# Attention over the scales: the second image's means and columns mostly on GpSimd, and a written-out ending for the last two items

## The chip, the cores and the metric

One core of a Trainium2 chip runs the whole program. The metric is the device time of one execution in microseconds (us). The engines are PE (TensorE), DVE (VectorE), ACT (ScalarE), POOL (GpSimd) and SP, which issues DMAs. Each works through its own instructions in order, and waits on semaphores for what other engines produce.

## The reference, cut to what matters

The program is four layers on an image batch of 2 x 128 x 64 x 64 in float32: a block of state-space layers, two attention layers over 4096 pixels, and an attention over scales. Only the last is changed:

```python
for i, scale in enumerate((1, 2, 4, 8)):
    if scale > 1:
        xs = x.reshape(b, c, h // scale, scale, w // scale, scale).mean(axis=(3, 5))
        f = bilinear_resize(conv3x3(xs, conv_w[i], conv_b[i]), h, w)
    else:
        f = conv3x3(x, conv_w[i], conv_b[i])
    feats.append(f)
xr = jnp.stack(feats, axis=1).transpose(0, 3, 4, 1, 2).reshape(b * h * w, 4, c)
qkv = xr @ attn_in_w.T + attn_in_b
q, k, v = (heads(t) for t in jnp.split(qkv, 3, axis=-1))      # 8 heads
scores = jnp.einsum('nhqd,nhkd->nhqk', q, k) / jnp.sqrt(jnp.float32(hd))
o = jnp.einsum('nhqk,nhkd->nhqd', softmax(scores), v)
res = o.transpose(0, 2, 1, 3).reshape(-1, 4, c) @ attn_out_w.T + attn_out_b + xr
normed = layernorm(res) * ln_g + ln_b                         # over the 128 channels
fused = normed.reshape(b, h, w, 4, c).transpose(0, 3, 4, 1, 2).reshape(b, 4 * c, h, w)
out = jnp.einsum('bchw,oc->bohw', fused, fus_w) + fus_b[None, :, None, None]
```

At every pixel four tokens, one for each scale, attend to each other, and a projection of all four gives the output.

## The kernel before, in words

The 128 channels lie on the partitions. The layer starts near 4233 us and runs to the end. An item is one image (b) and one of eight chunks of 512 pixels (c), so there are NI = 16 items, 0 to 7 of the first image and 8 to 15 of the second. The stage is under a manual schedule: each engine's order is the order in which the program issues. Nothing plans it; the function `period(n)` (L1273) writes it out by hand.

A period works on four items at once: o = n - 1 is normalised and fused, p = n gets its attention weights applied and its output mix, m = n + 1 its scores and soft maximum, r = n + 2 its features, convolution and projections. Some steps and their lines:

- `features(r)`, L1118: POOL makes the three coarse feature maps of a chunk from the columns `lo` and their vertical differences `di` (L1124, L1125, L1133, L1134).
- `conv(r)`, L1113: nine matmuls of the full-size convolution, in pieces along the period.
- `product` and `scores` of m: DVE multiplies k (PSUM) by q (L1157), PE sums over the heads (L1164).
- `weights` and `weighted` of p: for each key scale ti PE spreads the attention weights into a PSUM tile pw (L1199), and DVE multiplies it by v (L1206). `add_ov` (L1210) sums the four results: 0 + 1 on POOL after ti = 1, then 2 + 3 and 0 + 2 on DVE.
- `soft_max`, `soft_exp`, `soft_sum` of m (L1174 to L1192): DVE, ACT, DVE. They end in `at`.
- `mix_out(p)`: for each scale two matmuls into a po tile (L1219, L1220), which ACT evacuates twice, as the square sq (L1221) and as cen (L1222). The po, pqkv, pf and coarse-convolution tiles share one PSUM pool of three buffers.
- `variance`, `newton` and `factors` of p: PE sums the squares (pva, L1228), ACT takes logarithm, exponential and square (L1233, L1234, L1236), DVE (L1241), ACT (L1242) and DVE (L1243) refine the result, PE spreads it (prs, L1250). prs and pw are the same single buffer of four PSUM banks.
- `normalise` and `fuse` of the item before: DVE scales cen by prs (L1257), PE fuses the scales (pfus, L1264), ACT adds the bias (L1269), SP sends the chunk out (L1270).

Three steps are done once for an image, not for an item. `means(b)` (L1045): for scales 2, 4 and 8, DVE adds neighbouring columns into t1 (L1053, reading every second element) and neighbouring rows into sm (L1054), POOL clears the padded tile xs (L1056), ACT writes the scaled means into it (L1057). `coarse_conv` (L1060): nine matmuls on xs (L1069), ACT writes the result fl (L1075 or L1077). `columns(si)` (L1079): horizontal interpolation on DVE: differences df (L1085), copies at both edges (L1088, L1089), one multiply-add for each of the 2, 4 or 8 phases (L1092), the first and last row repeated (L1095, L1096), vertical differences di for scales 4 and 8 (L1100). For image 0 they run ahead of the periods. For image 1 they are put into periods by the table `extra`, whose hooks `more(k)` stand at fixed places of `period`: means in period 2 after soft_sum (hook 4), the coarse convolutions in periods 3 and 4 at hooks 1 and 3, the columns in period 5 at hook 4, ahead of mix_out.

prod, ov, sq, t1 and df take turns in six buffers of the tag "prod"; sm and fl of a scale share one buffer.

Periods run from n = -2 to 16. In the last two most steps have no item: period 15 normalises and fuses item 14 and applies the weights of item 15, period 16 normalises and fuses item 15.

Of the kernel before, what the change touches and what calls it, by code (L numbers as in the profile page):

```python
# [6 lines left out]
F32 = mybir.dt.float32  # L7
AF = mybir.ActivationFunctionType
ALU = mybir.AluOpType
# [4 lines left out]
B, C, H, W = 2, 128, 64, 64  # L14
N = H * W
P = 128
# [13 lines left out]
NS = len(SCALES)  # L30
# [37 lines left out]
def tile_conv_seq(ctx: ExitStack, tc, x, consts, vecs, wemb, wlay, wconv, wdt, wqkv, wsmall, wms, out):  # L68
    nc = tc.nc
# [46 lines left out]
    with tc.manual_schedule(), ExitStack() as s:  # L116
# [4 lines left out]
        sp = scans.enter_context(tc.tile_pool(name="l0s", bufs=1, side="right"))  # L121
# [91 lines left out]
        NI, NST, NSL = len(items), 8, 32  # L213
        st = [{} for _ in items]
# [3 lines left out]
        def has(i):  # L218
            return 0 <= i < NI
# [676 lines left out]
        sp = s.enter_context(tc.tile_pool(name="ats", bufs=1, reuse_waits="tile"))  # L896
        psa = s.enter_context(tc.tile_pool(name="atpa", bufs=2, reuse_waits="tile", space=PSUM))
        psm = s.enter_context(tc.tile_pool(name="atpm", bufs=1, reuse_waits="tile", space=PSUM))
        for now in range(NALL + LAG + 10):
            r, u = divmod(now, NU)  # L900
            w = now % 8
# [70 lines left out]
    with ExitStack() as s, tc.manual_schedule():  # L972
        sp = s.enter_context(tc.tile_pool(name="mss", bufs=1, reuse_waits="tile"))
# [50 lines left out]
        for si in (2, 3):  # L1024
            wgt[si] = sp.tile([P, SCALES[si]], F32, name=f"wgt{si}")
            for k in range(SCALES[si]):
                w = (k + 0.5) / SCALES[si] - 0.5
# [5 lines left out]
        NI = len(items)  # L1033
        st = [{} for _ in items]
        low = {}
        coarse = {}
# [6 lines left out]


        def means(b):  # L1045
            prev, off = xt[:, b], 1
            for si in range(1, NS):
                sc_ = SCALES[si]
                hh = H // sc_
                t1 = sp.tile([P, 2 * hh, hh], F32, name=f"t1_{si}", tag="prod", bufs=6)  # L1050
                sm = sp.tile([P, hh, hh], F32, name=f"sm_{si}", tag=f"fl{si}")
                e = off + 2 * hh
                nc.vector.tensor_tensor(t1, prev[:, off:e, off:e:2], prev[:, off:e, off + 1 : e : 2], ALU.add)  # L1053
                nc.vector.tensor_tensor(sm, t1[:, 0 : 2 * hh : 2, :], t1[:, 1 : 2 * hh : 2, :], ALU.add)  # L1054
                xs = coarse["xs", si] = sp.tile([P, hh + 2, hh + 2], F32, name=f"xs_{si}", tag=f"xs{si}")
                nc.gpsimd.memset(xs, 0.0)  # L1056
                nc.scalar.activation(xs[:, 1 : hh + 1, 1 : hh + 1], sm, AF.Copy, scale=1.0 / (sc_ * sc_))  # L1057
                prev, off = sm, 0

        def coarse_conv(si, r0):  # L1060
# [15 lines left out]
            else:  # L1076
                nc.scalar.activation(dst, src, AF.Identity, bias=v1("conv_b3", si))  # L1077

        def columns(si):  # L1079

            sc_ = SCALES[si]
            hh, half = H // sc_, sc_ // 2
            fl = coarse["fl", si]
            df = sp.tile([P, hh, hh - 1], F32, name=f"df_{si}", tag="prod", bufs=6)
            nc.vector.tensor_tensor(df, fl[:, :, 1:], fl[:, :, : hh - 1], ALU.subtract)  # L1085
            lo = sp.tile([P, hh + 2, W], F32, name=f"lo_{si}", tag=f"lo{si}")
            mid = lo[:, 1 : hh + 1, :]
            nc.vector.tensor_copy(mid[:, :, :half], fl[:, :, 0:1].to_broadcast([P, hh, half]))  # L1088
            nc.vector.tensor_copy(mid[:, :, W - half :], fl[:, :, hh - 1 : hh].to_broadcast([P, hh, half]))  # L1089
            for kk in range(half, half + sc_):  # L1090
                end = kk + sc_ * (hh - 2) + 1
                nc.vector.scalar_tensor_tensor(  # L1092
                    mid[:, :, kk:end:sc_], df, (kk + 0.5) / sc_ - 0.5, fl[:, :, : hh - 1], ALU.mult, ALU.add
                )
            nc.vector.tensor_copy(lo[:, 0, :], lo[:, 1, :])  # L1095
            nc.vector.tensor_copy(lo[:, hh + 1, :], lo[:, hh, :])  # L1096
            di = None
            if si > 1:
                di = sp.tile([P, hh + 1, W], F32, name=f"di_{si}", tag=f"di{si}")
                nc.vector.tensor_tensor(di, lo[:, 1:, :], lo[:, : hh + 1, :], ALU.subtract)  # L1100
            low[si] = lo, di


# [104 lines left out]
        def add_ov(eng, i, a, b):  # L1208
            o = st[i]["ov", a]
            eng.tensor_tensor(o, o, st[i].pop(("ov", b)), ALU.add)  # L1210
# [62 lines left out]
        def period(n, extra):  # L1273
            o, p, m, r = n - 1, n, n + 1, n + 2

            def do(i, f, *a):
                if has(i):
                    f(i, *a)

            def more(k):  # L1280
                for f, a in extra.get((n, k), ()):
                    f(*a)


            do(r, features)
            do(r, conv, (0, 1))
            for ti in range(NS):
                do(m, product, ti)
                if ti == 0:
                    do(o, normalise)  # L1290
                do(p, weights, ti)
                if ti + 2 < NS:
                    do(m, project, 1, ti + 2)
                if ti > 0:
                    do(m, scores, ti - 1)
                do(p, weighted, ti)
                if ti == 1 and has(p):
                    add_ov(nc.gpsimd, p, 0, 1)
                if ti == 0:
                    do(o, fuse, range(NS))  # L1300
                do(r, conv, ((), (2, 3), (4, 5), (6, 7))[ti])
                more(ti)
            do(m, scores, NS - 1)

            if has(p):
                add_ov(nc.vector, p, 2, 3)
                add_ov(nc.vector, p, 0, 2)
            do(m, soft_max)
            do(r, conv, (8,))
            do(r, conv_out)  # L1310
            for si in range(NS):
                do(m, project, 2, si)
            do(m, soft_exp)
            do(m, soft_sum)
            more(4)
            for si in range(NS):
                do(p, mix_out, si)
            more(5)

            do(p, variance)  # L1320
            for si in range(NS):
                if si == 2:
                    do(p, newton)
                do(r, project, 0, si)
            do(r, project, 1, 0)
            do(p, factors)
            do(r, project, 1, 1)
            more(6)

        means(0)  # L1330
        for r0 in (0, 16):
            coarse_conv(1, r0)
        coarse_conv(2, 0), coarse_conv(3, 0)
        for si in range(1, NS):
            columns(si)
        last = NCH - 3
        extra = {
            (last - 3, 4): [(means, (1,))],
            (last - 2, 1): [(coarse_conv, (1, 0))], (last - 2, 3): [(coarse_conv, (1, 16))],
            (last - 1, 1): [(coarse_conv, (2, 0))], (last - 1, 3): [(coarse_conv, (3, 0))],  # L1340
            (last, 4): [(columns, (si,)) for si in range(1, NS)],
        }
        for n in range(-2, NI + 1):
            period(n, extra)


# [79 lines left out]
```

## Time and profile before

| | us |
|---|---|
| median of 3 runs | 5029.0 (5028.12 to 5030.46) |
| profiled execution, its own time | 5032.79 |
| its span, first to last instruction | 5031.0 |
| PE busy | 4671.6 (93%) |
| DVE busy | 4024.3 (80%) |
| ACT busy | 2367.4 (47%) |
| POOL busy | 2309.9 (46%) |
| mean granted clock of PE | 0.948 of full speed |

A line of the timeline gives start, duration, engine, line of the program, operation, output <- inputs, sizes and a count of instructions; square brackets hold the idle time just ahead of it and what ended it. A line of windows gives, for a stretch of time, its length and each engine's busy time with its number of instructions, the granted clock, the share of DMA and the rate. Line numbers are those of the kernel before.

### The profile page before, as it was taken

To read this page: it belongs to the slowest core of one execution; us is meant where nothing else is said; L and a number is where in the kernel's file an instruction comes from. 1 tells how busy PE (TensorE), PEld (TensorE's weight loads), DVE (VectorE), ACT (ScalarE), POOL (GpSimd) and SP (SyncE) were. 2 spreads that over 40 slices of the span, in tenths; PEclk is the share of its full clock that TensorE was granted. 3 is DMA by queue.
4 is the path that set the end of the run, shared out by engine and by line. 5 is a ranking of instruction groups with operands and counts; after the bars stand their busy time and mean duration, and the time that the engine had idled before them with its cause. 6 is when DMAs were issued, how large, how long until landed. Compare 5 with 4: busy or idle time off the path is not lost.

```text
span 5031.0 us, 48923 instructions
## 1 busy us (share of the span) xinstructions
PE 4671.6 (93%) x14797; PEld 2244.9 (45%) x14797; DVE 4024.3 (80%) x4284; ACT 2367.4 (47%) x3221; POOL 2309.9 (46%) x1948
## 2 busy tenths in 40 slices
PE   5889999999988899899999999999999999999997
PEld 1222222222222222366667766666666666333332
DVE  6999999999999999788886677667766775767775
ACT  4677777777777777522222222333333332223332
POOL 3777776666777777513332233233333333323331
PEclk8898889988999989899999999999999999999998
DMA  6333333332333333224444344434443442000000
GB/s 162 68 68 69 69 71 71 71 68 63 71 68 68 72 71 70 62 65 108 109 110 126 105 112 110 117 98 110 114 100 97 112 111 70 5 5 7 7 7 7
DMA packets 242343, 386.24 MB, mean 77 GB/s; under 512 B 88592, under 2 KB 88992, under 8 KB 233632
## 3 DMA queue, kind: packets, MB, share of 16 engines
q1 hardware_dynamic: 192928, 315.94, 25.9%
q10 hardware_dynamic: 49152, 67.17, 5.4%
q8 instruction: 118, 1.93, 0.2%
q14 instruction: 145, 1.19, 0.1%
HBM read 101.02 MB, written 13.37 MB: 23 GB/s over the span
## 4 chain that ended last, share of the span: by engine, by line
PE 49%; POOL 24%; issue 12%; DVE 9%; ACT 2%; DMA 2%; SPq 1%; ACTq 0%; DVEq 0%; POOLq 0%
POOL h L410 19%; PE po L804 15%; PE pq L754 15%; PE pa L652 2%; PE pf L1113 2%; DVE tr L784 2%; PE pqkv L1140 2%; POOL dtu L370 1%; PE pw L1199 1%; POOL z L433 1%; PE pb L652 1%; PE pfus L1264 1%; PE psc L1164 1%; PE po L1220 1%; DVE prod L1157 1%
## 5 line engine op out<-in xcount | busy, mean ns | idle before, releaser
L791 POOL COPY pt<-tr 32x512 f32<-32x512 f32 x1024 | 649.0, 634 | 1440.2 <-DVE tr L784 711.7
L407 DVE TENSOR_TENSOR_SCAN h<-da,carry,h 128x512 f32<-128x512 f32 x1024 | 1241.6, 1266 | 59.9 <-ACT da L396 31.0
L410 POOL TENSOR_TENSOR h<-h,cb 128x2048 f32<-128x2048 f32 x256 | 1161.4, 4537 | 20.9 <-POOL carry L409 0.4
L754 PE MATMUL pq<-k,q 128*128 128x512 f32 x2048 | 962.8, 593 | 9.1 <-DVE sc L759 6.8
L804 PE MATMUL po<-pt,vt 128*128 128x256 f32 x4096 | 967.3, 379 | 2.8 <-DMA pt<-tr 2.8
L769 ACT ACTIVATE sc<-sc,nm 128x2048 f32<-128x2048 f32 x256 | 510.5, 1995 | 912.0 <-DVE nm L765 675.4
L759 DVE TENSOR_SCALAR_CACHE_REDUCE sc<-pq 128x1024 f32<-128x1024 f32 x512 | 625.0, 1222 | 366.7 <-PE pq L754 345.4
L804 PEld LDWEIGHTS po<-pt,vt 128*128 128x128 f32 x4096 | 779.1, 190 | 295.6 <-issue 208.3
L396 ACT ACTIVATE da<-dtb,am 128x512 f32<-128x512 f32 x1024 | 681.6, 684 | 231.1 <-DVE h L407 210.2
L389 DVE TENSOR_TENSOR h<-bb,pdu 128x2048 f32<-128x2048 f32 x256 | 581.8, 2273 | 85.8 <-PE py L422 29.3
L784 DVE STREAM_TRANSPOSE tr<-sc 128x2048 f32<-128x2048 f32 x256 | 591.7, 2311 | 63.2 <-DMA pt<-tr 53.9
L422 PE MATMUL py<-h,sel 128*32 128x512 f32 x2048 | 511.4, 643 | 1.6 <-POOL h L410 1.6
L754 PEld LDWEIGHTS pq<-k,q 128*128 128x128 f32 x2048 | 382.8, 190 | 284.8 <-issue 246.1
L383 PE MATMUL pdu<-dtu,fsel 128*128 128x512 f32 x512 | 325.3, 722 | 116.0 <-DVE h L389 113.8
L422 PEld LDWEIGHTS py<-h,sel 128*32 128x32 f32 x2048 | 115.2, 118 | 415.3 <-issue 409.9
L310 PE MATMUL pu<-xn,wu 128*128 128x512 f32 x512 | 246.7, 615 | 2.6 <-ACT xn L300 1.7
L383 PEld LDWEIGHTS pdu<-dtu,fsel 128*128 128x128 f32 x512 | 95.9, 214 | 321.8 <-DVE h L389 199.2
L409 POOL COPY carry<-h 128x4 f32<-128x4 f32 x256 | 47.5, 185 | 395.8 <-DVE h L407 393.9
L1206 DVE TENSOR_TENSOR ov<-v,pw 128x2048 f32<-128x2048 f32 x64 | 146.2, 2285 | 68.6 <-PE pw L1199 68.6
L1140 PE MATMUL pqkv<-f,ws 128*128 128x512 f32 x384 | 189.5, 618 | 3.0 <-DVE prod L1157 2.3
L1210 POOL TENSOR_TENSOR ov<-ov 128x2048 f32<-128x2048 f32 x16 | 72.6, 4536 | 257.7 <-DVE ov L1206 257.7
L370 POOL TENSOR_TENSOR dtu<-dt,u 128x1024 f32<-128x1024 f32 x32 | 75.1, 2346 | 191.9 <-ACT dt L364 191.9
(245 smaller groups left out, 5254.4 us busy)
## 6 DMA issues: line engine op xcount, KB each, us to landing
pt<-tr SPq DMA_DIRECT2D x2048, 64.0 KB, 2.0
dtb<-dt SPq DMA_DIRECT2D x1024, 64.0 KB, 2.0
pt<-tr ACTq DMA_DIRECT2D x1024, 64.0 KB, 2.2
bb<-dr SPq DMA_DIRECT2D x128, 256.0 KB, 4.4
cb<-dr SPq DMA_DIRECT2D x128, 256.0 KB, 4.7
uw<-ufold SPq DMA_DIRECT2D x12, 576.0 KB, 4.3
uw<-dkept SPq DMA_DIRECT2D x20, 288.0 KB, 3.0
xt<-in_x SPq DMA_DIRECT2D x16, 256.0 KB, 4.7
```

The lines of the kernel that those rows point to most:

```text
L383: nc.tensor.matmul(pdu, lhsT=four(s_ % 4), rhs=st[i]["dtu"][:, s_ // 4, :], start=True, stop=True)
L389: nc.vector.tensor_tensor(h, st[i]["bc", 0], pdu.unsqueeze(1).to_broadcast([P, 4, CH]), ALU.mult)
L396: nc.scalar.activation(da, st[i]["dtb", s_], AF.Exp, scale=am[items[i][1]][:, j, gg, m : m + 1])
L407: nc.vector.tensor_tensor_scan(h[:, m, :], da, h[:, m, :], carries[b, l][:, j, gg, m : m + 1], ALU.mult, ALU.add)
L410: nc.gpsimd.tensor_tensor(h, h, st[i]["bc", 1], ALU.mult)
L422: nc.tensor.matmul(py[r : r + 32, :], lhsT=sel, rhs=st[i]["h", s_ + k][:, m, :], start=(m == 0), stop=(m == 3), tile_position=(0, r),)
L754: nc.tensor.matmul(pq[:, i, :], lhsT=sta["q", r, grp][:, it * P : (it + 1) * P], rhs=sta["k"][:, at : at + CH], start=True, stop=True)
L759: nc.vector.tensor_scalar(dst, pq, 1.0, None, ALU.mult, ALU.max, accum_out=sta["mx"][:, c2 : c2 + 1])
L769: nc.scalar.activation(sc, sc, AF.Exp, bias=nm, scale=scale, accum_out=sm[:, hh : hh + 1])
L784: nc.vector.transpose(tr, sta.pop(("sc", r, blk, hh)).rearrange("p (t r f) -> p r t f", r=NB, f=32))
L791: nc.gpsimd.tensor_copy(dst, src)
L804: nc.tensor.matmul(sta["po", r, grp], lhsT=sta["vt"][:, jt, :], rhs=rhs, start=(jt == 0), stop=(jt == N // P - 1))
```

## The change

Three things. `means(1)` is wholly on POOL: its six sums, the clearing, and the three scales. `means(0)` stays as it was. `columns` is cut into three parts: part 0 makes the differences df and the edge copies, part 1 the interpolations, part 2 the edge rows and di. For image 1 parts 0 and 2 are on POOL and part 1 stays on DVE; they stand at hooks 3, 4 and 5 of period 5. For image 0 everything stays on DVE, now scale by scale through the three parts, in the order of before. And periods 15 and 16 are replaced by `ending`: period 14 no longer ends in factors(14); the four weights and weighted steps of item 15 come first, then factors, normalise and fuse of item 14, then item 15's additions on DVE, the last of them in four pieces of 512, its mix_out, variance, newton and factors, and its normalise in four pieces, each followed by its fuse matmul.

```diff
 def means(b):
+    eng = nc.gpsimd if b else nc.vector
...
-        nc.vector.tensor_tensor(t1, prev[:, off:e, off:e:2], prev[:, off:e, off + 1 : e : 2], ALU.add)
-        nc.vector.tensor_tensor(sm, t1[:, 0 : 2 * hh : 2, :], t1[:, 1 : 2 * hh : 2, :], ALU.add)
+        eng.tensor_tensor(t1, prev[:, off:e, off:e:2], prev[:, off:e, off + 1 : e : 2], ALU.add)
+        eng.tensor_tensor(sm, t1[:, 0 : 2 * hh : 2, :], t1[:, 1 : 2 * hh : 2, :], ALU.add)
...
-        nc.scalar.activation(xs[:, 1 : hh + 1, 1 : hh + 1], sm, AF.Copy, scale=1.0 / (sc_ * sc_))
+        if b:
+            nc.gpsimd.tensor_scalar(xs[:, 1 : hh + 1, 1 : hh + 1], sm, 1.0 / (sc_ * sc_), None, ALU.mult)
+        else:
+            nc.scalar.activation(xs[:, 1 : hh + 1, 1 : hh + 1], sm, AF.Copy, scale=1.0 / (sc_ * sc_))
...
-def columns(si):
+def columns(b, si, part):
+    eng = nc.gpsimd if b else nc.vector
...
+    if part == 0:
+        df = coarse["df", si] = sp.tile([P, hh, hh - 1], F32, name=f"df_{si}", tag="prod", bufs=6)
+        eng.tensor_tensor(df, fl[:, :, 1:], fl[:, :, : hh - 1], ALU.subtract)
+        lo = coarse["lo", si] = sp.tile([P, hh + 2, W], F32, name=f"lo_{si}", tag=f"lo{si}")
+        mid = lo[:, 1 : hh + 1, :]
+        eng.tensor_copy(mid[:, :, :half], fl[:, :, 0:1].to_broadcast([P, hh, half]))
+        eng.tensor_copy(mid[:, :, W - half :], fl[:, :, hh - 1 : hh].to_broadcast([P, hh, half]))
+        return
+    lo = coarse["lo", si]
+    if part == 1:
+        mid, df = lo[:, 1 : hh + 1, :], coarse.pop(("df", si))
+        for kk in range(half, half + sc_):
...
+                mid[:, :, kk:end:sc_], df, (kk + 0.5) / sc_ - 0.5, fl[:, :, : hh - 1], ALU.mult, ALU.add
...
+        return
+    eng.tensor_copy(lo[:, 0, :], lo[:, 1, :])
+    eng.tensor_copy(lo[:, hh + 1, :], lo[:, hh, :])
...
+        eng.tensor_tensor(di, lo[:, 1:, :], lo[:, : hh + 1, :], ALU.subtract)
...
-    do(p, factors)
+    if p != NI - 2:
+        do(p, factors)
...
+def ending():
+    o, p = NI - 2, NI - 1
+    for ti in range(NS):
+        weights(p, ti)
+        weighted(p, ti)
+        if ti == 1:
+            add_ov(nc.gpsimd, p, 0, 1)
+    factors(o)
+    normalise(o)
+    fuse(o, range(NS))
+    add_ov(nc.vector, p, 2, 3)
+    a, b = st[p]["ov", 0], st[p].pop(("ov", 2))
+    for si in range(NS):
+        nc.vector.tensor_tensor(a[:, si, :], a[:, si, :], b[:, si, :], ALU.add)
+    for si in range(NS):
+        mix_out(p, si)
+    variance(p)
+    newton(p)
+    factors(p)
+    w = st[p]
+    for si in range(NS):
+        nc.vector.tensor_tensor(w["cen"][:, si, :], w["cen"][:, si, :], w["prs"][:, si, :], ALU.mult)
+        fuse(p, (si,))
...
-    (last, 4): [(columns, (si,)) for si in range(1, NS)],
+    (last, 3): [(columns, (1, si, 0)) for si in range(1, NS)],
+    (last, 4): [(columns, (1, si, 1)) for si in range(1, NS)],
+    (last, 5): [(columns, (1, si, 2)) for si in range(1, NS)],
...
-for n in range(-2, NI + 1):
+for n in range(-2, NI - 1):
     period(n, extra)
+ending()
```

More of the change, by code (lines that the diff above doesn't have):

```diff
@@ L1083, in columns @@
             fl = coarse["fl", si]
[L1084 to L1096, printed above, removed]
+            if part == 0:
[10 more added lines that the diff above has]
+                for kk in range(half, half + sc_):
+                    end = kk + sc_ * (hh - 2) + 1
+                    nc.vector.scalar_tensor_tensor(
+                        mid[:, :, kk:end:sc_], df, (kk + 0.5) / sc_ - 0.5, fl[:, :, : hh - 1], ALU.mult, ALU.add
+                    )
+                return
+            eng.tensor_copy(lo[:, 0, :], lo[:, 1, :])
+            eng.tensor_copy(lo[:, hh + 1, :], lo[:, hh, :])
             di = None
@@ L1099, in columns @@
                 di = sp.tile([P, hh + 1, W], F32, name=f"di_{si}", tag=f"di{si}")
-                nc.vector.tensor_tensor(di, lo[:, 1:, :], lo[:, : hh + 1, :], ALU.subtract)
+                eng.tensor_tensor(di, lo[:, 1:, :], lo[:, : hh + 1, :], ALU.subtract)
             low[si] = lo, di
@@ L1334, in tile_conv_seq @@
         for si in range(1, NS):
-            columns(si)
+            for part in range(3):
+                columns(0, si, part)
         last = NCH - 3
```

## The prediction

> **What bounds the kernel now.** I read the page's chain of waits first, then windows between equal instructions of the last stage, then the single instructions where a window is long. Over the whole span the chain lies on PE for 49% and on POOL for 24%, but POOL's part is L410, in a stage that the change leaves alone. What counts is the last 800 us. There I cut windows from one item's variance matmul (L1228, pva) to the next: one turn of `period`.
>
> ```profile
> core 0: us, PE busy (x) PEld busy (x) DVE busy (x) ACT busy (x) POOL busy (x), PEclk, DMA share, GB/s
> 4334.05:4376.45 42.40, 41.37 (x147) 14.26 (x146) 31.43 (x20) 14.62 (x23) 13.17 (x14) 1.00 0.02 7
> 4376.45:4427.60 51.15, 43.44 (x147) 14.67 (x147) 36.47 (x26) 16.09 (x26) 15.36 (x18) 0.93 0.02 6
> 4578.19:4629.80 51.61, 44.52 (x147) 15.26 (x146) 42.72 (x48) 14.69 (x23) 14.65 (x14) 0.90 0.02 6
> 4968.85:5031.00 62.15, 34.94 (x97) 11.12 (x96) 21.07 (x12) 13.04 (x21) 4.51 (x1) 0.75 0.02 8
> ```
>
> The first row is an undisturbed period: PE is busy 41.37 of 42.40 us, so PE bounds it, and DVE and POOL have 11 and 29 us to spare. The second holds the second image's means: 8.75 more. The third holds its columns: 9.2 more (51.61 - 42.40). The fourth is the ending, with PE idle 27 us: a serial chain. These three rows are all that the change can win in.
>
> Means:
>
> ```profile
> 4412.76 1.02 PE L1220 MATMUL po<-ov,wc 128*128 128x512 f32 x2
> ...
> 4417.05 2.25 DVE L1053 TENSOR_TENSOR t<-xt 128x2048 f32<-128x2048 f32 x1
> ...
> 4420.65 1.61 ACT L1057 ACTIVATE xs<-sm 128x1024 f32<-128x1024 f32 x2 [6.70 <-DVE sm L1054]
> ...
> 4423.89 2.07 PE L1219 MATMUL po<-f,kc 128*128 128x512 f32 x2 [6.68 <-ACT cen L1222]
> ```
>
> ACT's first scale waits for DVE's sums with mix_out's evacuations queued behind it; they free PE's three po buffers, so PE idles 6.68 and comes back at half clock (2.07 against 1.02).
>
> Columns:
>
> ```profile
> 4576.38 1.15 DVE L1085 TENSOR_TENSOR df<-fl 128x992 f32<-128x992 f32 x1
> ...
> 4589.69 0.68 DVE L1241 SCALAR_TENSOR_TENSOR nt<-pva,nt 128x512 f32<-128x512 f32 x1
> ...
> 4591.91 2.09 PE L1250 MATMUL prs<-rs,kc 32*128 32x512 f32 x8 [7.09 <-DVE rs L1243]
> ```
>
> DVE works 13.4 us on columns; newton (L1241) stands behind. In the undisturbed period it starts 3.98 after pva, here 11.50, 7.5 late; PE waits 7.09 and loses 3.2 more in four groups at half clock (prs, pqkv, and pf 3.17 against 1.88).
>
> Ending:
>
> ```profile
> 4974.30 0.69 DVE L1243 TENSOR_TENSOR rs<-rs,nt 128x512 f32<-128x512 f32 x1 [0.79 <-ACT nt L1242]
> ...
> 4981.70 2.29 DVE L1206 TENSOR_TENSOR ov<-v,pw 128x2048 f32<-128x2048 f32 x1 [2.21 <-PE pw L1199]
> 4987.63 2.29 DVE L1206 TENSOR_TENSOR ov<-v,pw 128x2048 f32<-128x2048 f32 x1 [3.65 <-PE pw L1199]
> ...
> 4998.07 4.69 DVE L1210 TENSOR_TENSOR ov<-ov 128x2048 f32<-128x2048 f32 x2
> ...
> 5022.04 5.17 PE L1264 MATMUL pfus<-cen,wfus 128*128 128x512 f32 x8 [2.39 <-DVE cen L1257]
> ```
>
> One PSUM tile serves prs and pw, so PE and DVE alternate from 4975 to 4998.
>
> **What the Trainium skill says.** "SBUF — State Buffer", Who interferes with whom: a DVE instruction with two SBUF inputs and a GpSimd instruction that reads SBUF exclude each other for the whole instruction; with one SBUF input DVE is free of it. The trace agrees:
>
> ```profile
> 49.83 2.34 POOL L370 TENSOR_TENSOR dtu<-dt,u 128x1024 f32<-128x1024 f32 x1 [28.37 <-ACT dt L364]
> ...
> 49.96 2.62 DVE L202 SCALAR_TENSOR_TENSOR uhi<-raw,uhi 128x384 f32<-128x384 f32 x1
> ```
>
> L202 takes 2.62 where its neighbour of the same shape takes 0.56: it waited for POOL to end. L1206, one PSUM input, stays at 2.29 beside POOL. "TensorE: Matmul & The Clock Gate", Part 1: after an idle window of some 3.4 us the clock halves; the 2.09 for prs above, usually 1.14, agrees. "GPSIMD Engine Reference", 7: a read step above 8 bytes costs half more; the means step over 2 floats, 8 bytes, at the edge, and no row here shows that step on POOL.
>
> **Means, step by step.** Removed: DVE's six sums and ACT's three scales, and with them the 8.75. Added: the same nine instructions on POOL, after its add 0+1, which ends at 4401.6; POOL then has idle time until features at 4418 (and these wait some 20 us before a projection needs them). POOL's prices: L1210 4.54 for 2048, L370 2.35 for 1024, so 0.16 plus 2.14 ns an element. The first sum is 4.54 (bounds 4.54, since no row of this size is shorter, and 6.8 with the half of section 7; I take 4.54, the step being not above 8), the second 2.35, memset 1.06, the scale over 1024 between 1.6 (ACT's two together) and 3.4 (four times L1124's 0.86 for 256), I take 2.9. The rest is 3 us. All of it is hidden as work; the exclusion is not. The add 2+3 (L1210, two SBUF inputs) is ready at 4406.5. POOL's first sum ends at 4406.2 and its second holds until 4408.6; DVE adds to 4410.9; POOL's waiting scale takes 2.9; DVE adds 0+2 from 4413.7 to 4416.0, before 4411.15. PE needs that at 4412.76 (L1220): 3.2 idle, plus 1.1 at half clock. Gain 8.7 - 4.3 = **4.4**; bounds 3.0 (another sum gets between) and 8.2 (no meeting). The first sum's reused buffers wait for score matmuls already past; in the next period DVE's first ov waits for POOL's small sums, due 4431, done near 4424.
>
> **Columns, step by step.** Differences and edge copies go to POOL after its add 0+1 (ends 4561.0), where it is idle until 4580: 2.3 us for 992 elements, less for the rest. I price this at nothing: it may hold DVE's add 2+3 by some 0.3, which has about 1.4 before PE asks; without the cover the interpolations start later by these 2.3. DVE keeps the 14 interpolations (L1092): 2.29, 2.54, 2.65, of which the last two were stretched by POOL's features running beside them; their free pace is 0.43 and 0.125 each, so 2.3 + 1.7 + 1.0 = 5.0, in a gap of 5.7 before newton is due. But part 2 runs on POOL between them: four edge rows, some 0.2 each, and two differences, 0.16 + 1088 x 2.14 ns = 2.5 and 1.4. If the first gets in before the last scale's interpolations, these end near 4584.7 in place of 4581.5, newton's L1243 (two SBUF inputs) then waits for the second: 2.7 late against the undisturbed 4584.65. Some 0.4 of that is taken up by q's evacuation; half clock adds 0.9. Cost 3.2, gain 9.2 - 3.2 = **6.0**; bounds 3.0 (4.5 late with full clock loss) and 8.7 (all in the gap). The next item's features come some 6 us later on POOL, 30 us before PE needs them; SP is untouched.
>
> **Ending, step by step.** weights(15, 0) needs only `at` (ready 4968.6) and runs in PE's idle time. L1206 follows L1243 at 4975.0, ends 4977.3. Three rounds of 2.16 (start of a half-clock pw to L1206) + 2.29 + 0.05 = 4.5 each: 4990.8. factors(14) 2.2, normalise 2.3: 4995.3. fuse(14) 4.9: 5000.3; beside it DVE adds 2+3 (2.3) and the chunks (0.7 each), done at 5000.5 with the first at 4998.4; POOL's add is done at 4986.4. mix_out then at full clock as in the undisturbed period, 6.9: pva at 5007.2, before 5011.57. Gain 4.3 (2.5 if mix_out is half clocked, 5.6 if fuse is full clocked, 3.6). Tail: prs to end of fuse is 9.35 before. Now prs 1.8, first quarter of L1257 0.7, four fuse quarters of 5.17 in all, each quarter of DVE's covered by PE: 7.7. Gain 1.7 (1.5 to 2.9). Together **6.0**, bounds 4 and 8.
>
> **Sum.** 4.4 + 6.0 + 6.0 = 16.4. The profiled execution took 5032.8 (span 5031.0), so 5016.4; the median is 3.8 lower: **5012.6**.
>
> **Rivals.** B, the engines miss each other: if POOL's first sum takes over 4.9, DVE's add 2+3 gets in ahead of the second sum, and loses under 1; likewise the interpolations may end before the difference starts. 8.2 + 8.5 + 6.0 = 22.7: 5006.3. For it: margins of 0.3 us decide. C, the exclusion and half clock cost nearly all: 2.5 + 2.5 + 4.0 = 9.0: 5020.0. For it: POOL and DVE took turns op by op in the columns above, and PE fell to half clock after each long idle. D, the new order of the ending brings nothing, as the same tile still makes PE and DVE take turns: 5018.6; against it, fuse(14) and the adds leave the chain. E, slower: the means' two-float step on POOL costs several times a plain row. Then each sum holds off DVE's add (two SBUF inputs) for its whole length. The 9.8 us of sum, sum and scale, at f times the price, push DVE's second add back by 9.8 x (f - 1); it decides from 16.4, f = 2.7; at 3.5 it is 24.5 more: 5037. Against it: section 7's half is far from that, and DVE's own strided L1053 costs no more than a plain row.
>
> **Numbers.** Forecast 0.53, B 0.20, C 0.17, D 0.05, E 0.05. A measurement here tells 0.2% from no change: 5018.9 is the bound, so faster has forecast, B and D, 0.78; same is C, 0.17; slower is E, 0.05. The range 5004.5 to 5020.5 takes in all but E and the outer bounds of B and C.
>
> **What would show it.** Right: the means' period near 46.8, the columns' near 45.6, PE's wait ahead of prs there under 3; L1210's add 2+3 drawn out beside POOL; last pva 4.3 earlier relative to the one before. Wrong: POOL's first sum well over 6.8; newton still 5 or more late; pw and L1206 alternating past 4992.

## The result, and the profile after

The changed kernel takes 5008.06 us (median of 5 runs, 5006.2 to 5011.36), the kernel before 5030.46 in the same comparison. The ratio is 0.9956, with a 95% interval of 0.9943 to 0.997: 22.4 us less, where 16.4 were forecast. The time lies inside the stated range, 4.5 below the predicted 5012.6. The gain is 6.0 more than forecast; the two differ since the kernel before measured 1.5 more here than in the runs that the prediction started from (5029.0).

The windows of the changed kernel, cut as those of before, from one variance matmul (pva, now L1240) to the next, and the last one to the end of the span:

```profile
4378.44:4421.12 42.68, 41.64 (x148) 14.18 (x147) 33.33 (x20) 14.17 (x23) 28.30 (x26) 1.00 0.02 7
4571.71:4614.12 42.41, 41.44 (x147) 14.26 (x146) 34.94 (x33) 14.62 (x23) 20.14 (x22) 1.00 0.02 7
4951.37:5008.80 57.43, 33.43 (x97) 10.99 (x96) 21.30 (x18) 13.04 (x21) 4.51 (x1) 0.73 0.02 9
```

The means' period went from 51.15 to 42.68, the columns' from 51.61 to 42.41, which is an undisturbed period to a hundredth. PE keeps its full clock in both. The ending went from 62.15 to 57.43. Gains of 8.5, 9.2 and 4.7 make 22.4. Two more terms in these two traces nearly cancel: the stage began 2.0 later in the profiled run after, and the period before the ending was 1.8 shorter (42.19 before, 40.38 after; more on that below). The spans differ by 22.2.

The means in the timeline of the changed kernel:

```profile
4403.57 3.67 POOL L1055 TENSOR_TENSOR t<-xt 128x2048 f32<-128x2048 f32 x1
...
4407.32 2.35 POOL L1056 TENSOR_TENSOR sm<-t 128x1024 f32<-128x1024 f32 x1
...
4408.53 6.33 DVE L1222 TENSOR_TENSOR ov<-ov 128x2048 f32<-128x2048 f32 x2
...
4410.76 3.70 POOL L1060 TENSOR_SCALAR xs<-sm 128x1024 f32<-128x1024 f32 x1
...
4414.91 1.12 PE L1232 MATMUL po<-ov,wc 128*128 128x512 f32 x2
```

DVE's two additions take 6.33 beside POOL (4.62 before). They end at 4414.86. PE wants the result at 4414.75 (4412.76 in the trace of before, and this period began 1.99 later), so it waits one or two tenths of a microsecond. The line of L1232 has no idle time in brackets: it was below what the view prints.

The columns:

```profile
4569.90 5.12 DVE L1103 SCALAR_TENSOR_TENSOR lo<-df,fl 128x992 f32<-128x992 f32 x14
...
4575.33 2.50 POOL L1112 TENSOR_TENSOR di<-lo 128x1088 f32<-128x1088 f32 x1
...
4578.43 1.14 PE L1262 MATMUL prs<-rs,kc 32*128 32x512 f32 x8
```

All 14 interpolations run in 5.12, their undisturbed pace. They are over at 4575.02, 0.3 before POOL comes to its first difference at 4575.33. PE's prs is on time, without idle time ahead of it, at 1.14: full clock. Before, it had waited 7.09.

The ending:

```profile
4957.43 2.28 DVE L1218 TENSOR_TENSOR ov<-v,pw 128x2048 f32<-128x2048 f32 x1
4959.77 2.09 PE L1211 MATMUL pw<-at,spread 32*128 32x512 f32 x8 [5.43 <-DVE ov L1218]
...
4970.92 2.29 DVE L1218 TENSOR_TENSOR ov<-v,pw 128x2048 f32<-128x2048 f32 x1 [2.21 <-PE pw L1211]
...
4977.77 6.05 PE L1276 MATMUL pfus<-cen,wfus 128*128 128x512 f32 x8 [2.41 <-DVE cen L1269]
...
4983.65 1.02 PE L1231 MATMUL po<-f,kc 128*128 128x512 f32 x2
...
4999.79 5.28 PE L1276 MATMUL pfus<-cen,wfus 128*128 128x512 f32 x8 [0.80 <-DVE cen L1365]
```

PE and DVE still take turns on the one four-bank tile, 4.5 us a round (three rounds from 4957.43 to 4970.92). The fuse of item 14 takes 6.05, longer than any before, most of it at half clock.

### The profile page after: what moved, and what is told of

Its sections match the earlier page's. It is cut to its first block, busy times and chain, and to the rows that moved or that the text cites. A ratio compares the mean times of both kernels' runs of the same rounds, so it can differ in the third digit from the quotient of the medians.

```text
span 5008.8 us, 48937 instructions
## 1 busy us (share of the span) xinstructions
PE 4665.6 (93%) x14797; PEld 2244.5 (45%) x14797; DVE 4013.3 (80%) x4267; ACT 2365.5 (47%) x3218; POOL 2338.1 (47%) x1974
## 4 chain that ended last, share of the span: by engine, by line
PE 52%; POOL 20%; issue 11%; DVE 9%; ACT 4%; DMA 2%; SPq 1%; ACTq 0%; DVEq 0%; POOLq 0%
POOL h L410 16%; PE po L804 15%; PE pq L754 15%; PE pa L652 2%; DVE tr L784 2%; PE pf L1125 2%; PE pqkv L1152 2%; PE py L422 2%; DMA pt<-tr 2%; PE pw L1211 1%; DVE h L407 1%; SPq L795 1%; PE pb L652 1%; PE pu L310 1%; PE pfus L1276 1%
```

## The experiments

**Each part undone by itself.** Three kernels, each the changed one with one part as before.

a1, means back on DVE and ACT:

```diff
-            eng = nc.gpsimd if b else nc.vector
+            eng = nc.vector
...
-                if b:
-                    nc.gpsimd.tensor_scalar(xs[...], sm, 1.0 / (sc_ * sc_), None, ALU.mult)
-                else:
-                    nc.scalar.activation(xs[...], sm, AF.Copy, scale=1.0 / (sc_ * sc_))
+                nc.scalar.activation(xs[...], sm, AF.Copy, scale=1.0 / (sc_ * sc_))
```

> The changed kernel with only the second image's means back on DVE and ACT. My theory, that the three parts are independent and each removes its own window: the means' period (pva to pva) goes from 42.7 back to 51.15, the columns' period and the ending stay, so 8.5 us longer than the changed kernel, near 5016.5. The rival, that the exclusion cost 4.3 us somewhere that the traces hide (gain of the part 4.4 only): near 5012.5.

a2, columns back on DVE:

```diff
-            (last, 3): [(columns, (1, si, 0)) for si in range(1, NS)],
-            (last, 4): [(columns, (1, si, 1)) for si in range(1, NS)],
-            (last, 5): [(columns, (1, si, 2)) for si in range(1, NS)],
+            (last, 4): [(columns, (1, si, part)) for si in range(1, NS) for part in range(3)],
```

(with `eng = nc.vector` in `columns`)

> The changed kernel with only the columns of the second image back on DVE, all at hook 4. Theory of independent parts: columns' period from 42.4 back to 51.6, so 9.2 us longer, near 5017.3. Rival, a cost of POOL's parts of columns given back in a later period (features late): less than 9.2, 6.0 by my prediction, near 5014.

a3, the old ending:

```diff
-        for n in range(-2, NI - 1):
+        for n in range(-2, NI + 1):
             period(n, extra)
-        ending()
```

(and `factors` again in every period)

> The changed kernel with periods 15 and 16 as before. From pva of item 14 to the end 57.4 goes back to 62.15: 4.7 us longer, near 5012.8. Rival: the 1.8 us that the trace shows in the period before (fuse at full clock, 3.60 in place of 4.82) belongs to the ending too, then 6.5 longer, near 5014.6; if it is the phase of the clock window, this kernel has the short fuse or the long one independently of the ending.

Measured: a1 5018.2 (ratio to the kernel before 0.9975, 0.9965 to 0.9985), a2 5016.44 (0.9969, 0.9956 to 0.9981), a3 5013.42 (0.9965, 0.9952 to 0.9978). Against the changed kernel's 5008.06 that is 10.1, 8.4 and 5.4 more, from separate comparisons whose intervals reach 5 to 7 us to either side. Their windows, from three traces (the means' period of a1, the columns' of a2, the ending of a3):

```profile
4373.59:4424.74 51.15, 43.44 (x148) 14.68 (x147) 36.47 (x26) 16.08 (x26) 15.37 (x18) 0.93 0.02 6
```

```profile
4568.37:4619.15 50.78, 43.69 (x148) 15.00 (x147) 42.71 (x48) 14.67 (x23) 14.65 (x14) 0.93 0.02 6
```

```profile
4951.63:5014.40 62.77, 35.53 (x97) 11.40 (x96) 21.07 (x12) 13.03 (x20) 4.51 (x1) 0.75 0.02 8
```

a1's window goes back to its old length. The other two come near theirs: 50.78 for 51.61, where the granted clock is 0.93 for 0.90, and 62.77 for 62.15. The two windows that a kernel does not undo stay, to 0.3 us. So the three parts are independent, and each gains what its window shows. The times agree with that, but can't show more: the stage's first pva comes anywhere from 4328.3 to 4336.3 in the eleven traces of the whole program, though nothing ahead of it was changed. a1 undoes the sums and the scales together, and no run tells what each of them is worth.

The 1.8 us in the period before the ending do not belong to the change. That period lasts 40.4 at a granted clock of 1.00 in the changed kernel, in a3 and in e6 (below), and 41.9 to 42.1 at 0.96 in the other seven changed ones, though the changed kernel and e5, for instance, are the same program up to its end. It goes with the granted clock, and why that differs from run to run is open. The ending is not free of this either: it lasts 57.2 to 58.1 in the six traces that have it, and 62.15 and 62.77 in the two with the old one.

**The meeting that the prediction priced, brought about.** In the changed kernel POOL's second sum starts 1.2 ahead of DVE's addition; the prediction had it start 0.3 ahead, and the whole of it in DVE's way. a4 moves POOL's sums 1.06 later:

```diff
+                if si == 1:
+                    xs = coarse["xs", si] = sp.tile([P, hh + 2, hh + 2], F32, name=f"xs_{si}", tag=f"xs{si}")
+                    nc.gpsimd.memset(xs, 0.0)
                 t1 = sp.tile([P, 2 * hh, hh], F32, name=f"t1_{si}", tag="prod", bufs=6)
...
-                xs = coarse["xs", si] = sp.tile([P, hh + 2, hh + 2], F32, name=f"xs_{si}", tag=f"xs{si}")
-                nc.gpsimd.memset(xs, 0.0)
+                if si > 1:
+                    xs = coarse["xs", si] = sp.tile([P, hh + 2, hh + 2], F32, name=f"xs_{si}", tag=f"xs{si}")
+                    nc.gpsimd.memset(xs, 0.0)
```

> The changed kernel with POOL's clearing of the largest padded means tile put ahead of the first sum, not behind the second: POOL's sums come 1.06 us later, so that the second sum starts just ahead of DVE's add 2+3 (ready at 4408.5), which is the meeting that the prediction priced. Prediction's theory (each POOL instruction that reads SBUF shuts DVE's two-input add out for its whole length, turn by turn): the add 2+3 ends near 4413.0, the scale takes the next turn to 4415.9, add 0+2 ends near 4418.2, PE waits 3.4 us ahead of L1232 in that period and loses up to 1 at half clock: means' period 46 to 47, near 5012. Rival (the one-input scale holds DVE up little, 0.7 us as the changed kernel's trace suggests): add 0+2 ends near 4416, PE waits 1.3, period near 44, 5009.5.

Measured: 5010.02 (0.9957, 0.9942 to 0.9971), means' period 43.68. From its timeline:

```profile
4404.73 2.34 POOL L1059 TENSOR_TENSOR sm<-t 128x1024 f32<-128x1024 f32 x1
...
4404.93 7.34 DVE L1226 TENSOR_TENSOR ov<-ov 128x2048 f32<-128x2048 f32 x2
...
4407.17 4.70 POOL L1064 TENSOR_SCALAR xs<-sm 128x1024 f32<-128x1024 f32 x1
...
4412.32 1.12 PE L1236 MATMUL po<-ov,wc 128*128 128x512 f32 x2 [1.00 <-DVE ov L1226]
```

The second sum now shuts out DVE's first addition in full: started at 4404.93, it gets going at about 4407, when the sum ends. But the scale, whose record lies across most of the second addition, adds only 0.7: 7.34 is 4.62 + 2.0 + 0.7. The second addition by itself takes 3.01 here and in the changed kernel, where one takes 2.29 undisturbed. The rival won; DVE does not wait out the 2.9 that the prediction gave the scale.

**The prices by themselves.** m1 leaves out the whole computation. POOL runs each instruction twice alone, and twice beside four DVE additions of 128x2048 with both inputs in SBUF, both released by one ACT instruction. One such pair of segments (the lines left out are one tiny POOL instruction on `src`, which makes POOL wait for it):

```python
src = start()
...
f(src); f(src)
src = start()
...
for k in range(4):
    nc.vector.tensor_tensor(d, src, oth, ALU.add)
f(src); f(src)
```

> None of the reference is computed: the output is zeros. POOL runs pairs of one instruction alone, and then beside four DVE adds of 128x2048 with both inputs in SBUF (2.29 each alone, 9.2 for four). Prediction's theory, exclusion for the whole instruction for whatever POOL reads: the four adds grow by the whole time of the POOL instructions that they meet, whether these have one input or two, and a sum over pairs of neighbouring columns takes 4.5 to 6.8. What the changed kernel's trace suggests instead: the sum over pairs takes 3.67; a two-input instruction stretches the adds by its whole length; a scale over 1024 takes some 2.6 to 3 alone and stretches them by only 0.7; a clearing by nothing.

Measured, the line of DVE's four additions beside two sums of two tiles, beside two scales of 1024, and alone:

```profile
22.20 17.50 DVE L86 TENSOR_TENSOR d<-src,oth 128x2048 f32<-128x2048 f32 x4 [20.81 <-ACT src L131]
...
94.73 10.57 DVE L86 TENSOR_TENSOR d<-src,oth 128x2048 f32<-128x2048 f32 x4 [9.92 <-ACT src L131]
...
215.24 8.90 DVE L86 TENSOR_TENSOR d<-src,oth 128x2048 f32<-128x2048 f32 x4 [2.04 <-ACT src L131]
```

| two POOL instructions | alone, us | four additions beside them | growth over 8.90 |
|---|---|---|---|
| sum of two tiles, 2048 | 9.06 | 17.50 | 8.60 |
| sum of neighbouring rows, 1024 | 4.71 | 13.15 | 4.25 |
| copy, 2048 | 3.84 | 12.28 | 3.38 |
| scale into padded rows, 1024 | 5.65 | 10.57 | 1.67 |
| scale, 2048 | 10.81 | 15.77 | 6.87 |
| clearing, 2048 | 3.67 | 8.90 | 0 |

Two-input sums shut DVE's additions out for nearly their whole length, and so does a copy, which has one input. A scale lets DVE through for about 2.0 of its length each time (10.81 - 6.87 and 5.65 - 1.67, halved), and so the 1024 one costs DVE 0.8 out of 2.8. Clearing costs nothing. So it is not the number of POOL's inputs that decides, as the second half of my expectation had it. Why a scale lets DVE through for those 2.0 is open. The sum over pairs of columns, alone, took 3.65, where a plain sum of that size takes 4.49; a sum with a step of four elements took 2.05 for 1024, where the plain one takes 2.3.

**What lateness of newton costs.** c1 leaves part 0 on POOL and puts part 2 on DVE:

```diff
-            eng.tensor_copy(lo[:, 0, :], lo[:, 1, :])
-            eng.tensor_copy(lo[:, hh + 1, :], lo[:, hh, :])
+            nc.vector.tensor_copy(lo[:, 0, :], lo[:, 1, :])
+            nc.vector.tensor_copy(lo[:, hh + 1, :], lo[:, hh, :])
...
-                eng.tensor_tensor(di, lo[:, 1:, :], lo[:, : hh + 1, :], ALU.subtract)
+                nc.vector.tensor_tensor(di, lo[:, 1:, :], lo[:, : hh + 1, :], ALU.subtract)
```

> The changed kernel with part 2 of the second image's columns (edge rows and differences) on DVE, ahead of newton; part 0 stays on POOL. DVE then works 5.1 + about 2.9 us in a gap of 5.8 ahead of newton. Prediction's model of lateness (PE pays the lateness less 0.4[...]): newton 2.2 late, period 42.4 + 1.8 = 44.2, or 45 with half clock; near 5010. Rival, that only POOL's two-input differences matter and DVE's own time there is free: 42.4, 5008.

c2 keeps everything where the changed kernel has it, but in the order of scales 4, 8, 2:

```diff
-            (last, 4): [(columns, (1, si, 1)) for si in range(1, NS)],
-            (last, 5): [(columns, (1, si, 2)) for si in range(1, NS)],
+            (last, 4): [(columns, (1, si, 1)) for si in (2, 3, 1)],
+            (last, 5): [(columns, (1, si, 2)) for si in (2, 3, 1)],
```

> The changed kernel with the interpolations in the order of scales 4, 8, 2, and POOL's part 2 in the same order, so that POOL's first difference (two inputs, 2.5 us) comes free while DVE still has the two long interpolations of scale 2. Prediction's step for the columns (a difference that gets in between shuts DVE out for its length): one long interpolation takes 3.3 to 3.6 instead of 1.15, newton 1.5 to 2.5 late, period 43.5 to 45, near 5010. Rival, that DVE's instructions in a row keep POOL out as they seem to in the changed kernel: newton on time, 42.4, 5008.

Measured: c1 5011.95 (0.9961, 0.9948 to 0.9975), c2 5010.44 (0.9958, 0.9943 to 0.9973); these intervals do not tell them from the changed kernel, their windows do. First c1, its period and PE's wait, then c2, where POOL's difference comes while DVE is still interpolating:

```profile
4566.96:4611.73 44.77, 41.45 (x147) 14.27 (x147) 38.38 (x41) 14.73 (x23) 15.39 (x14) 1.00 0.02 6
4576.23 1.14 PE L1262 MATMUL prs<-rs,kc 32*128 32x512 f32 x8 [2.65 <-DVE rs L1255]
```

```profile
4569.52:4613.21 43.69, 41.45 (x148) 14.27 (x147) 37.00 (x31) 14.69 (x23) 20.89 (x22) 1.00 0.02 7
4567.71 7.45 DVE L1103 SCALAR_TENSOR_TENSOR lo<-df,fl 128x240 f32<-128x240 f32 x14
...
4570.23 2.49 POOL L1112 TENSOR_TENSOR di<-lo 128x1088 f32<-128x1088 f32 x1
```

In c1 newton's last step ends 2.76 late and the period grows by 2.36 over the 42.41 of the changed kernel; in c2 it ends 1.30 late and the period grows by 1.28. So PE pays the lateness, less 0.0 to 0.4. The half clock that the expectation allowed for did not come, even at 2.65 of idle time (prs 1.14, granted 1.00). c1 also tells the parts of the columns apart: 50.78 with all on DVE (a2), 44.77 with parts 1 and 2 there, 42.41 with part 1 alone. In c2 the interpolations take 7.45 for 5.12: the difference did shut DVE out once it got in, though it met a short interpolation and not, as expected, a long one. The exclusion is real in the columns too; the changed kernel escapes it by its order, and by 0.3 us.

**The one tile of the ending.** e5 takes the last item's weights through single PSUM banks, and moves item 14's normalise and fuse behind item 15's additions:

```diff
             for ti in range(NS):
-                weights(p, ti)
-                weighted(p, ti)
...
+                for si in range(NS):
+                    r = slice(32 * si, 32 * si + 32)
+                    bank = mmt("pwb")
+                    nc.tensor.matmul(
+                        bank, lhsT=spread[r, ti, :], rhs=st[p]["at"][r, :], start=True, stop=True, tile_position=(32 * si, 0)
+                    )
+                    nc.vector.tensor_tensor(ov[:, si, :], v, bank, ALU.mult)
...
             factors(o)
-            normalise(o)
-            fuse(o, range(NS))
             add_ov(nc.vector, p, 2, 3)
...
+            normalise(o)
             for si in range(NS):
                 mix_out(p, si)
             variance(p)
+            pf = mmt("pfb")
+            for si in range(NS):
+                nc.tensor.matmul(pf, lhsT=wfus[:, si, :], rhs=st[o]["cen"][:, si, :], start=(si == 0), stop=(si == NS - 1))
             newton(p)
```

(item 15's cen takes one of the six "prod" buffers; item 14's bias and store follow behind factors(15))

> The changed kernel with another ending: the last item's weights go through the three single PSUM banks that are free by then, each multiplied by v in a piece of 512, so that PE fills one bank while DVE reads another; item 14's factors, normalise and fuse come behind item 15's weights and additions, the fuse in PE's idle time before newton. Theory: the ending is bound by one four-bank tile for which PE and DVE take turns, 4 x 4.5 us. Then sixteen pieces of 0.62 are 9.9 in place of 18, and normalise and fuse of item 14 (some 7 us from prs to the first mix_out) leave the chain: last pva 26 to 29 after the one before in place of 39.2, total 10 to 13 less than the changed kernel, near 4997. Rival: DVE's own work bounds it (9.9 + adds 4.8 + smaller pieces), and the half clock of PE takes back the rest: 5 less, near 5003.

Measured: 4997.36 (0.9933, 0.9921 to 0.9946), faster than both kernels. From pva of item 14 to the next 31.91 (39.24 in the changed kernel; 26 to 29 expected), to the end 47.58. The ending's window, within it the stretch in which PE fills banks, and the first and the last of DVE's pieces:

```profile
4946.52:4994.10 47.58, 38.25 (x97) 15.06 (x96) 22.61 (x30) 13.04 (x21) 4.52 (x1) 0.78 0.03 11
4953.31:4965.00 11.69, 11.69 (x28) 6.28 (x32) 8.19 (x13) 0.00 (x0) 4.52 (x1) 0.51 0.00 0
```

```profile
4952.58 1.88 DVE L1356 TENSOR_TENSOR ov<-v,pwb 128x512 f32<-128x512 f32 x3
...
4966.56 0.69 DVE L1356 TENSOR_TENSOR ov<-v,pwb 128x512 f32<-128x512 f32 x1 [0.71 <-PE pwb L1353]
```

The total came as expected, but not in the expected way. The loop from the first to the last of DVE's multiplications by v took 14.7 and not 9.9; in the changed kernel it takes 15.8 (4957.43 to 4973.21). So the single banks won 1.1, where the expectation had 8. The rest of the 9.85 by which the ending is shorter lies behind the loop: 6.2 from its end to the last pva, where normalise and fuse of item 14 no longer stand ahead of mix_out, and 2.5 in the tail, where the fuse of item 14 fills PE's idle time and prs and the last fuse run at full clock (1.14 and 3.70 for 2.09 and 5.28). No run has the single banks or the new order alone. That the sum came out is in part luck.

In the second row of the windows PE's records leave no gap and the granted clock is 0.51, and DVE waits for PE. These matmuls have 32 rows (32*128 in the timeline). Two kernels ask whether that is why. Both add full-height matmuls into a tile that nothing reads:

```diff
                     nc.vector.tensor_tensor(ov[:, si, :], v, bank, ALU.mult)
+                    if ti == 0 and si == 2:
+                        for k in range(4):
+                            warm(CH)
+                    elif ti or si > 2:
+                        warm(P)
```

e6 is that edit; e7 is without its last two lines.

> The kernel with single banks in the ending, plus matmuls of full height (128 rows) into a spare PSUM tile that nothing reads: four of 512 columns in PE's idle time before the weights go on, then one of 128 columns behind each bank of weights. The weights' matmuls have 32 rows; in the kernel with single banks PE was 97% busy with them for 12 us and was granted half speed all the while. Theory: 32-row matmuls do not count as the activity that releases the clock, full-height ones do. Then a bank takes 0.3 + 0.2, DVE's 0.62 bounds the loop (9.9 in place of 14.7), mix_out runs at full clock: last pva some 26 after the one before in place of 31.9, total 5 to 6 less, near 4992. Rival: the clock does not answer to it; then the added matmuls only add, some 3 to 6 us more, near 5002.

> As the kernel that is kept warm, but with the four full-height matmuls in the idle time alone and none between the banks of weights. Theory (32-row matmuls do not count): the clock holds for one or two windows of 3.4 us and then falls to half in spite of a busy PE; pva 28 to 30 after the one before, near 4995. Rival (any busy PE keeps the clock once it is at full): as fast as with the full-height matmuls between, 26, near 4992.

Measured: e6 5013.94 (0.9964, 0.9952 to 0.9977), e7 4995.13 (0.9929, 0.9914 to 0.9944), which can't be told from e5. e6 is a miss, for its theory and for its rival. Its timeline, a bank and an added matmul at full clock, and later a bank at half:

```profile
4950.38 1.12 PE L1358 MATMUL pwb<-at,spread 32*128 32x512 f32 x2 [0.21 <-DVE ov L1361]
4951.43 0.49 PE L1350 MATMUL idle<-wfus,kc 128*128 128x128 f32 x2
...
4960.72 2.07 PE L1358 MATMUL pwb<-at,spread 32*128 32x512 f32 x2
```

One bank (x2) takes 1.12, and three together (x6, below) take 1.14 in e7: there the banks overlap, 0.4 a bank. With a full-height matmul behind each bank they come one by one, which costs some 0.7 a bank at full clock. That made PE, not DVE, the bound of the loop, and the clock fell all the same. e7, first three banks together, then a stretch behind the added full-height matmuls, then one a few microseconds on:

```profile
4950.71 1.14 PE L1358 MATMUL pwb<-at,spread 32*128 32x512 f32 x6
```

```profile
4955.70:4959.00 3.30, 3.30 (x11) 1.67 (x12) 3.27 (x6) 0.00 (x0) 0.00 (x0) 1.00 0.00 0
4960.00:4968.00 8.00, 8.00 (x23) 3.98 (x20) 5.36 (x9) 0.00 (x0) 4.51 (x1) 0.50 0.00 0
```

At full clock DVE is busy 3.27 of 3.30 and bounds the loop, as e5 had hoped. Then the clock falls, though PE's records leave no gap. The forecast for e7 held, 29.38 from pva to pva. What e5 and e7 show is that 32-row matmuls at this pace, a bank every 0.6 to 0.95 us, do not keep the clock. Whether that is for their height or because so few are under way at a time is not told apart, and how much full-height work would keep it is open, since e6 mixed both and lost it too.

## Why the prediction was right, and where it was off

The direction, the three windows and the bound (PE, with three serial stretches) were right. The costs that it priced in the first two were hardly paid: both gains lie above their stated bounds (8.5 over 8.2, 9.2 over 8.7), and the periods near 46.8 and 45.6 that it named as signs came to 42.68 and 42.41. That the time is inside the range owes much to the range being 16 us wide. By its own steps:

- Means, gain forecast 4.4, measured 8.5. The step that failed is the turn in "POOL's waiting scale takes 2.9; DVE adds 0+2 from 4413.7". The exclusion is there: the second sum held DVE up by 1.0 in the changed kernel, by 2.0 in a4. The scale is as long as priced (2.8 alone in m1), but held DVE up by 0.7, and the first sum took 3.67, not 4.54. These two are 3.1 of the 3.2 of idle time that I had priced; the 1.1 of half clock went with it. The bound that no such sum would be shorter than 4.54 was wrong: I took the plain row for a floor.
- Columns, 6.0 forecast, 9.2 measured. The free pace of the interpolations (5.0 forecast, 5.12 measured) and the gap were right. "If the first gets in before the last scale's interpolations" did not happen: of the two edge-row copies ahead of the difference the first took 0.88, beside DVE's interpolations, and the second 0.23, after them, and the difference began 0.3 after the last interpolation. Newton's last step ended 0.2 late in place of 2.7. c2 shows that the step was no fancy: in another order it costs 1.3. The 0.4 of lateness that PE does not pay came in c1; the 0.9 of half clock did not.
- Ending, 6.0 forecast, 4.7 measured. The chain to the fuse was right: 26.4 from pva to its start, 26.5 forecast. The terms mis-sized are fuse(14), 5.9 from its start to mix_out with 4.9 forecast (6.05 for the whole of it), and the tail from prs to the end of the last fuse, 8.2 with 7.7 forecast. 4.9 for the fuse and 1.8 for prs are what these steps took before (4.93 and 1.79). In the new order they meet another granted clock: 0.50 from 4958.63 to 4982.52, for 19 us of 32-row matmuls and idle time ahead of the fuse and most of the fuse itself.
- Of the rivals, B comes nearest: 22.7 forecast for it, 22.4 measured, 5006.3 against 5008.06. Its columns happened as it said. Its means did not: DVE did not get in ahead of the second sum, it only waited less for that sum and for the scale. So B's number is in part luck. C and D have no support, and E fell on the first POOL line of the trace (3.67): the strided sum is cheaper on POOL than the plain one. I gave B too little: with margins of 0.3 us the two cases should have had equal chances.

The Trainium skill, "SBUF — State Buffer", Who interferes with whom, says that the side which comes second is fully blocked. The runs agree for sums and copies (17.50 and 12.28 for 8.90 above), and not for the scale, where the measurement decides. "GPSIMD Engine Reference", 7, prices a read step above 8 bytes, in kernels for GpSimd's own cores, at half more; the sum with a step of 16 bytes took 2.05, less than the plain 2.3, so that price does not hold for this addition.

## What to carry to other kernels

A side job that delays a bounding engine costs what the window between two equal instructions shows: the wait, and in some windows half clock after it. Moved to an engine with idle time in that very stretch, it can be all but free (columns 42.41 for an undisturbed 42.40, means 42.68), as far as the two engines do not shut each other out. Ask of each moved instruction not only how long it is but how long it holds the other engine, measured for that kind of instruction; and where two engines miss each other by 0.3 us, write down both outcomes as equals. Where two engines take turns on one buffer, look at the work that waits behind the turns before splitting the buffer: in e5 the split shortened the turns by 1.1, and most of the other 8.7 lie where item 14's steps were moved out of the way.

## What the runs showed of the hardware that was not expected

- A POOL sum over pairs of neighbouring elements is faster than one over two plain tiles: 3.65 against 4.49 for 2048.
- A POOL scale takes 2.7 ns an element (2.78 for 1024), nearly three times a copy (1.89 for 2048), but shuts DVE's two-input additions out for only 0.8 of its 2.8 (1024), or 3.4 of its 5.4 (2048).
- A PE whose records of 32-row matmuls leave no gap was granted half clock (0.50 over 8 us in e7, 0.51 over 12 in e5).
- 32-row matmuls for different banks overlap (1.14 for three banks, 1.12 for one); with full-height matmuls between them they did not, some 0.7 us more for each bank at full clock.
